# Score maxima of an attention kernel: half of a PSUM tile reduced by itself, and a few DMAs queued behind others

## The chip, the cores and the metric

The kernel runs on one core of a Trainium2 chip. The metric is the device time of one execution in microseconds (us), the lower the better. The core has TensorE (PE, with its weight loads shown as PEld), VectorE (DVE), ScalarE (ACT), GpSimd (POOL), and SyncE (SP), which here issues all the DMAs. Each engine works through its own instruction stream; semaphores order the streams against each other.

## The reference

A layer norm, grouped-query attention and a feed-forward with ternary weights, on x of 8 batches by 1024 tokens by 256 features, all in float32. There are 16 query heads and 4 key heads of 16 features each.

```python
q = rope(ln(x) @ Wq);  k = rope(ln(x) @ Wk);  v = ln(x) @ Wv
scores = einsum("bhqd,bhkd->bhqk", q, k) / sqrt(256)
p = softmax(scores)                      # over 1024 keys
x = x + ln((p @ v) @ Wo)
x = x + ln(ln(x) @ (ternary(W) * alpha).T + bias)
```

A softmax needs the largest score of each query before its exponentials can be taken safely. The kernel finds the true maxima by computing the scores twice: once to find the maxima, and once, transposed and with the maxima subtracted, for the exponentials.

## The kernel before, in words

**Blocks.** The 8192 tokens are cut into 16 units of 512 queries. A unit has 4 blocks, so there are 64 blocks, numbered `i`; a block is 512 queries of four heads (in the last unit, 128 queries of all sixteen) against all 1024 keys. `k_st` holds the stacked keys of a batch in three rotating buffers, `q_st` the stacked queries of a unit in two. Each is split in a high and a low float32r part, stacked over 64 partition rows; two heads lie in the two halves of the 128 partitions, so that a matmul over rows 0 to 63 and one over rows 64 to 127 can run side by side.

**Maxima.** `max_scores(v)` (L558) emits the maxima's matmul number `v`, of 2048. Two of them (`part` 0 and 1, each 128 queries by 512 keys) fill one PSUM tile `sm` of 128 x 2 x 512 float32, one bank for each half; the pool `ps_mx` has two such tiles. After part 1 one DVE reduction (L590) takes the maximum over both halves, 1024 values for each query, into a column of `mx`. Only block 0, whose 16 tiles hold two heads rather than two halves of one, keeps two maxima for each tile (L586, into `mx_half`), because its keys arrive in two lots; they are joined at its end (L588).

**Shift rows.** When the 16 tiles of a block are reduced, `shift_split` (L597) splits the maxima into high and low parts (two small DVE instructions, L603 and L162). Later `shift_rows` (L606) transposes them on PE (`pm`), copies them on ACT (`mh`), and two DMAs (L619) put them into rows 48 and 49 and rows 112 and 113 of the block's `q_st`. There they multiply constant rows of -1 in `k_st`, so that the second score matmul subtracts the maximum. The block's exponentials cannot begin before those rows have landed.

**Exponentials.** `exp_one(s)` (L636) emits one transposed score matmul (`se`, L628; 128 keys by 512 queries, pool `ps_e` with three tiles) and one exponential on ACT (L643). There are 32 of these in a block. `av_piece` (L655) multiplies the exponentials by `v_aug` (values and a column of ones), which makes the output and the denominators.

**The order.** PE, DVE and ACT follow the program's order as written out by hand; POOL does so during the start, and later, like SP always, follows the order that the tile framework's scheduler gives it. The program's main loop goes through `windows()` (L1010): a window has 3 exponentials, or 2 at the end of a block. `window()` (L1052) emits them in turn with as many maxima matmuls: `se`, `sm`, `se`, `sm`, `se`, `sm`; then `parts_of_step` (L1029) emits pieces of other work that a table gives to this step (projection of later units, the tail of earlier ones, shift rows), and then the `av` matmuls of two windows earlier. The maxima run ahead of the exponentials by `maxima_by` (L1006), 40 to 48 matmuls. Since a window has three maxima matmuls and a tile takes two, a window often ends with one half of a tile filled, and the next window fills the other half.

**The start.** A second table (L952 to L978) gives pieces of units 1 and 2 to steps -10 to 9. The pieces that matter here: `third("kt")` (L419) rotates and splits the keys of unit 2 on POOL, sends them to DRAM in 4 DMAs (L430) and gathers them into `k_st` in 6 (`stack_keys`, L481). `stack_queries(1)` (L537) gathers the queries of unit 1 from DRAM into `q_st` with 6 DMAs of 256 KB (L542), and fills constant rows with two more (L146).

Of the kernel before, what the change touches and what calls it, by code (L numbers as in the profile page):

```python
# [8 lines left out]
F32 = mybir.dt.float32  # L9
F32R = mybir.dt.float32r  # L10
AF = mybir.ActivationFunctionType
ALU = mybir.AluOpType
AX = mybir.AxisListType
# [3 lines left out]
P = 128  # L17
# [4 lines left out]
UT = 4  # L22
# [6 lines left out]
def kernel(  # L29
# [29 lines left out]
    nc = tc.nc  # L59
# [5 lines left out]
    NK = S // P  # L65
# [9 lines left out]
    small = ctx.enter_context(tc.tile_pool(name="small", bufs=4))  # L75
# [31 lines left out]
    for src, lo, n in ((w_q, 0, D), (w_k, D, DK), (w_v, ROT, DK)):  # L107
        nc.sync.dma_start(
            out=wqkv[:, :, lo : lo + n], in_=src.rearrange("(c p) n -> p c n", p=P)
# [51 lines left out]
    def split_lo(eng, lo, src, hi):  # L161
        eng.tensor_tensor(lo, src, hi.bitcast(F32), ALU.subtract)  # L162
# [20 lines left out]
    def psum(shape, name, dtype=F32):  # L183
        if spare[0]:
            spare[0] += 1
            if spare[0] % 5 < 2:
                return ps_mx.tile(shape, dtype, tag="sm", name=name)
        return ps_e.tile(shape, dtype, tag="se", name=name)
# [360 lines left out]
    mx = {}  # L549

    def block_queries(i, r2=slice(None)):

        u, j = divmod(i, G)
        if u < NU - 1:
            return q_st[u % 2][:, j, r2, :]
        return q_st[u % 2][:, :, r2, j * P : (j + 1) * P]

    def max_scores(v):  # L558


        i, k = divmod(v // 2, 2 * NK)
        u, part = i // G, v % 2
        if i == 0:
            a, ch, t, r2 = 1 - part, k // NK, k // 2 % UT, k % 2
        else:
            a, ch, t, r2 = 1 - k % 2, part, k // 4, k // 2 % 2
        queries = block_queries(i, r2)
        queries = queries[:, t * P : (t + 1) * P] if u < NU - 1 else queries[:, t]
        if part == 0:
            sm[0] = ps_mx.tile([P, 2, 512], F32, tag="sm", name=f"sm_{i}_{k}")  # L570
            if k == 0:
                mx[i] = small.tile([P, 2, UT, 2], F32, tag="mx", name=f"mx_{i}")
            if k == 0 and i == 0:
                mx["half"] = small.tile([P, 2, 2, UT, 2], F32, tag="mx0", name="mx_half", bufs=1)
        rows = slice(64 * a, 64 * a + 64)
        nc.tensor.matmul(  # L576
            sm[0][:, part, :],
            queries[rows],
            k_st[(u // UPB) % 3][rows, r2, ch * 512 : (ch + 1) * 512],
            start=True,  # L580
            stop=True,
        )
        if part == 0:
            return
        if i == 0:
            nc.vector.tensor_reduce(mx["half"][:, ch, ::-1, t, r2], sm[0], AX.X, ALU.max)  # L586
            if k == 2 * NK - 1:
                nc.vector.tensor_tensor(mx[0], mx["half"][:, 0], mx["half"][:, 1], ALU.max)  # L588
        else:
            nc.vector.tensor_reduce(mx[i][:, a, t, r2 : r2 + 1], sm[0], AX.XY, ALU.max)  # L590
        if k == 2 * NK - 1:
            shift_split(i)
            due.append((v // 4 + (1 if i < 2 else 2), i))

    sm, mhl = {}, {}

    def shift_split(i):  # L597

        m = mx.pop(i)
        hl = mhl[i] = small.tile([P, 2, 2, 2 * UT], F32R, tag="mhl", name=f"mhl_{i}")  # L600
        order = "(r t)" if i // G < NU - 1 else "(t r)"
        hi, lo = (hl[:, :, l].rearrange(f"p a {order} -> p a t r", r=2) for l in range(2))
        nc.vector.tensor_copy(hi, m)  # L603
        split_lo(nc.vector, lo, m, hi)

    def shift_rows(i):  # L606

        hl = mhl.pop(i)
        pm = psum([8 * UT, P], f"pm_{i}", F32R)
        nc.tensor.transpose(pm, hl.rearrange("p a l x -> p (a l x)"), ident_r)  # L610
        mh = work.tile([8 * UT, P], F32, tag="mh", name=f"mh_{i}")
        nc.scalar.copy(mh, pm.bitcast(F32))
        n = 4 * UT
        for a in range(2):
            row = 64 * a + NROW
            dst = block_queries(i)[row : row + 2].bitcast(F32)
            if len(dst.shape) == 4:
                dst = dst.rearrange("l j c t -> l (j c) t")
            nc.sync.dma_start(out=dst, in_=mh[n * a : n * a + n, :])  # L619


    es, av_ps, av_sb, d_av = {}, {}, {}, {}
# [13 lines left out]
    def exp_one(s):  # L636

        n, (a, r2) = s // 4, divmod(s % 4, 2)
        i, kt = divmod(n, NK)
        e = es[n, r2, a] = ep.tile([P, UQ], F32, tag="e", name=f"e_{i}_{kt}_{r2}_{a}")  # L640
        sc = ps_e.tile([P, 512], F32, tag="se", name=f"se_{i}_{kt}_{r2}_{a}")
        exp_scores(n, r2, a, sc)
        nc.scalar.activation(e, sc, AF.Exp, scale=1.0 / D**0.5)  # L643

    def exp_two(n, r2):

        i, kt = divmod(n, NK)
        sc = ps_mx.tile([P, 2, 512], F32, tag="sm", name=f"se_{i}_{kt}_{r2}")
        for a in range(2):
            exp_scores(n, r2, a, sc[:, a, :])  # L650
        for a in range(2):
            e = es[n, r2, a] = ep.tile([P, UQ], F32, tag="e", name=f"e_{i}_{kt}_{r2}_{a}")
            nc.scalar.activation(e, sc[:, a, :], AF.Exp, scale=1.0 / D**0.5)
# [17 lines left out]
    def av_out(i):  # L671

        u, j = divmod(i, G)
        a = av_sb[u, j] = avp.tile([P, UQ], F32, tag="avsb", name=f"avsb_{i}")
        if i < NU * G - 1:
            nc.scalar.copy(a, av_ps[0])
        else:
            half = UQ // 2
            nc.scalar.copy(a[:, :half], av_ps[0][:, :half])
            nc.vector.tensor_copy(a[:, half:], av_ps[0][:, half:])  # L680
        if u < NU - 1:
            if j == 0:
                d_av[u] = dram.tile([H, 32, UQ], F32, tag="d_av", name=f"d_av_{u}")
            nc.sync.dma_start(out=d_av[u][HKV * j : HKV * (j + 1)], in_=a)
# [199 lines left out]
    def at(step, f, *args):  # L884
        assert step >= -START
        todo.setdefault(step, []).append((f, args))
# [59 lines left out]
    def second(name, *args):  # L946
        return lambda: getattr(projects[1], name)(*args)

    def third(name, *args):
        return lambda: getattr(projects[2], name)(*args)  # L950

    for k, fs in enumerate((  # L952
        [second("x", 1, 0), second("x", 1, 1), second("kv", 0)],
        [second("kv", 1), (pick, "q", 0, 0, 1), (pick, "q", 0, 1, 1), second("v"),
         second("rotate_k"), second("split_k")],
        [(pick, "q", 1, 0), (keep_warm, 1)],
        [(keep_warm, 3), second("k"), (keep_warm, 4), (pick, "k", 1, 0), (pick, "k", 1, 1),
         (keep_warm, 2)],
        [(pick, "q", 1, 1), second("q_product", 0), third("stats", 0),
         third("norm", 0, nc.scalar)],  # L960
        [second("q_product", 1), third("stats", 1), third("hi", 0, nc.scalar), third("lo", 0),
         (pick, "q", 2, 0)],
        [(pick, "q", 2, 1), third("norm", 1, nc.scalar), third("hi", 1, nc.scalar),
         third("lo", 1), (keep_warm, 3), (fill_constant_parts, 1)],
        [third("x", 0, 0), (pick, "q", 3, 0), (keep_warm, 3)],
        [third("x", 0, 1), (pick, "q", 3, 1), second("rotate_q", 0), (keep_warm, 2)],
        [third("x", 1, 0), third("x", 1, 1), second("split_q", 0)],
        [third("kv_and_dram"), second("rotate_q", 1)],
        [third("v"), second("split_q", 1), second("q_to_dram")],
        [third("kt")],  # L970
        [],
        [(fill_constant_parts, 2)],
        [],
        [third("q", 0)],
        [],
        [third("q", 1), (stack_queries, 1)],
        [third("q_to_dram")],
    )):  # L978
        for f in fs:
            at(k - START, *(f if isinstance(f, tuple) else (f,)))  # L980
# [25 lines left out]
    def maxima_by(s):  # L1006

        return s + 4 * START + 2 * sum(s >= k for k in (28, 36, 52, 68))
# [18 lines left out]
    maxima = [0]  # L1027
# [24 lines left out]
    def window(i, s, size, late):  # L1052
        if done:
            av_out(done.pop())
        if late:
            for r2 in range(2):
                exp_two(s // 4, r2)
        else:
            end = min(maxima_by(s + size), 4 * NSTEP)
            for q in range(max(size, end - maxima[0])):  # L1060
                if q < size:
                    exp_one(s + q)
                if maxima[0] < end:
                    max_scores(maxima[0])
                    maxima[0] += 1
        behind.append((i, s, size))
        for n in range(s // 4, (s + size) // 4):
            parts_of_step(n)
        av_windows(1 if late else 2)
# [135 lines left out]
```

## Time and profile before

| | |
|---|---|
| median of three runs | 1734.97 us (1734.68 to 1735.65) |
| the profiled execution's own time | 1735.28 us |
| its span, first to last instruction | 1733.1 us |
| mean granted TensorE clock | 0.983 |
| PE busy / DVE busy / ACT busy / POOL busy | 1602.1 / 1398.1 / 1271.0 / 836.0 us |
| maxima reductions on DVE (L590) | 1008, 1190.5 us busy, 1218 ns each |
| maxima matmuls (L576) / exponentials' score matmuls (L628) | 2048 / 2048 |
| exponentials on ACT (L643) | 2000, 1055.9 us busy, 602 ns each |

"Busy" is the time in which at least one instruction of the engine was under way. Two matmuls over different halves of the rows can be under way at once, so a PE that looks busy can still be held up: a stalled matmul over one half of the rows is hidden by another that is running over the other half. Idle time is therefore only a part of what PE loses. A waiting line such as "A <- B" gives the time in which A's engine had nothing under way until B released it; PEld lines are of the weight load that stands ahead of a matmul.

### The profile page before, as it was taken

To read this page: it belongs to the slowest core of one execution; us is meant where nothing else is said; L and a number is where in the kernel's file an instruction comes from. 1 tells how busy PE (TensorE), PEld (TensorE's weight loads), DVE (VectorE), ACT (ScalarE), POOL (GpSimd) and SP (SyncE) were. 2 spreads that over 40 slices of the span, in tenths; PEclk is the share of its full clock that TensorE was granted. 3 is DMA by queue.
4 is the path that set the end of the run, shared out by engine and by line. 5 is a ranking of instruction groups with operands and counts; after the bars stand their busy time and mean duration, and the time that the engine had idled before them with its cause. 6 is when DMAs were issued, how large, how long until landed. Compare 5 with 4: busy or idle time off the path is not lost.

```text
span 1733.1 us, 35758 instructions
## 1 busy us (share of the span) xinstructions
PE 1602.1 (92%) x14200; PEld 834.1 (48%) x14200; DVE 1398.1 (81%) x1752; ACT 1271.0 (73%) x2479; POOL 836.0 (48%) x1239
## 2 busy tenths in 40 slices
PE   7969999999999999999999999999999999999997
PEld 5534454444544445454454544545454544444444
DVE  6848778888788888878888788888978887888874
ACT  4637777777687777868777777877777786877775
POOL 5522447274453637346374644737455362333354
PEclk8879999999999999999999999999999999999999
DMA  4330424225151332515124151412414141140100
GB/s 131 66 78 32 83 73 87 63 76 97 41 101 43 82 82 61 104 39 98 51 74 96 54 102 46 90 58 78 84 48 95 45 87 51 33 82 32 40 14 25
DMA packets 86071, 117.88 MB, mean 68 GB/s; under 512 B 12089, under 2 KB 50809, under 8 KB 85753
## 3 DMA queue, kind: packets, MB, share of 16 engines
q1 hardware_dynamic: 85904, 115.60, 28.9%
q8 instruction: 112, 1.84, 0.5%
q14 instruction: 55, 0.44, 0.1%
HBM read 68.65 MB, written 45.88 MB: 66 GB/s over the span
## 4 chain that ended last, share of the span: by engine, by line
PE 34%; DVE 13%; POOL 4%; ACT 4%; issue 1%; DMA 1%; SPq 0%; POOLq 0%; ACTq 0%; DVEq 0%
PE av L663 13%; DVE mx L590 10%; PE se L628 10%; PE sm L576 4%; ACT e L643 3%; PE pa L283 2%; PE pf L283 1%; PE pq L283 1%; PE pt_ot L267 1%; DMA dq<-hlq 1%; DVE bnst L237 1%; PE pkv L283 1%; PE pt_xt L267 1%; POOL hlq L162 1%; DVE mhl L603 0%
## 5 line engine op out<-in xcount | busy, mean ns | idle before, releaser
L590 DVE TENSOR_REDUCE mx<-sm 128x1 f32<-128x1024 f32 x1008 | 1190.5, 1218 | 285.5 <-PE sm L576 242.2
L643 ACT ACTIVATE e<-se 128x512 f32<-128x512 f32 x2000 | 1055.9, 602 | 301.3 <-PE sm L576 238.5
L576 PE MATMUL sm<-k_st,q_st 64*128 64x512 f32 x2048 | 736.2, 449 | 45.7 <-DVE mx L590 41.8
L628 PE MATMUL se<-q_st,k_st 64*128 64x512 f32 x2048 | 685.8, 434 | 19.3 <-DMA q_st<-mh 18.3
L663 PE MATMUL av<-e,v_aug 128*32 128x256 f32 (+3 forms) x8096 | 591.7, 392 | 0.0
L628 PEld LDWEIGHTS se<-q_st,k_st 64*128 64x128 f32 x2048 | 330.8, 186 | 368.3 <-ACT e L643 217.3
L576 PEld LDWEIGHTS sm<-k_st,q_st 64*128 64x128 f32 x2048 | 324.5, 186 | 156.7 <-DVE mx L590 125.0
L663 PEld LDWEIGHTS av<-e,v_aug 128*32 128x32 f32 x8096 | 184.3, 109 | 192.6 <-issue 145.7
L241 POOL TENSOR_SCALAR lnsc<-mv 128x2 f32<-128x2 f32 (+1 forms) x134 | 25.8, 193 | 453.6 <-DVE mv L239 448.7
L737 POOL TENSOR_TENSOR xn<-xn,a 128x512 f32<-128x512 f32 x30 | 38.4, 1280 | 129.0 <-DMA a<-d_rec 115.1
L798 POOL TENSOR_TENSOR a<-a,bias_bc 128x512 f32<-128x512 f32 x30 | 39.0, 1300 | 117.2 <-ACT a L797 117.2
L242 POOL TENSOR_TENSOR lnsc<-lnsc,mhalf 128x2 f32<-128x2 f32 (+1 forms) x134 | 92.9, 694 | 0.9
L162 POOL TENSOR_TENSOR hl<-xn,hl 128x512 fp32r<-128x512 f32 x60 | 76.4, 1285 | 0.5
L253 POOL TENSOR_SCALAR xn<-x,lnsc 128x256 f32<-128x256 f32 x116 | 64.9, 568 | 3.4
L297 POOL TENSOR_TENSOR t<-q_rot,sin_q_sb 128x512 f32<-128x512 f32 x31 | 39.7, 1282 | 32.1 <-ACT q_rot L439 32.1
L764 ACT COPY a<-pa 128x512 f32<-128x512 f32 x30 | 17.6, 586 | 45.6 <-issue 45.6
L283 PE MATMUL pq<-xt,wqkvh 128*128 128x256 f32 x256 | 46.1, 304 | 2.8 <-ACT e L643 2.8
L237 DVE BATCH_NORM_STATS2 bnst<-a 128x6 f32<-128x256 f32 x120 | 44.6, 413 | 4.7 <-POOL a L798 4.7
L283 PE MATMUL pa<-woh,hl 128*128 128x256 f32 x240 | 47.0, 298 | 0.2 <-ACT e L643 0.2
L237 DVE BATCH_NORM_STATS2 bnst<-x 128x6 f32<-128x256 f32 x124 | 45.9, 412 | 1.1 <-DMA x<-in_L_attn_x 1.1
L267 PE MATMUL pt_xt<-ident_r,xs 128*128 128x128 f32 x256 | 33.4, 260 | 12.7 <-ACT e L643 11.1
L283 PEld LDWEIGHTS pq<-xt,wqkvh 128*128 128x128 f32 x256 | 36.3, 197 | 14.6 <-ACT e L643 13.2
(156 smaller groups left out, 1320.0 us busy)
## 6 DMA issues: line engine op xcount, KB each, us to landing
q_st<-dq SPq DMA_DIRECT2D x90, 256.0 KB
dq<-hlq SPq DMA_DIRECT2D x60, 256.0 KB
d_av<-avsb SPq DMA_DIRECT2D x60, 256.0 KB
x<-in_L_attn_x SPq DMA_DIRECT2D x15, 512.0 KB
xn<-d_av SPq DMA_DIRECT2D x30, 256.0 KB
a<-d_rec SPq DMA_DIRECT2D x30, 256.0 KB
xr<-in_L_attn_x SPq DMA_DIRECT2D x15, 512.0 KB
out_x<-a SPq DMA_DIRECT2D x30, 256.0 KB
```

The lines of the kernel that those rows point to most:

```text
L162: eng.tensor_tensor(lo, src, hi.bitcast(F32), ALU.subtract)
L237: nc.vector.bn_stats(st[:, t, :], src[:, t, :])
L242: nc.gpsimd.tensor_tensor(sc[:, 1, :], sc[:, 1, :], mhalf[:, :n], ALU.pow)
L253: eng.tensor_scalar(dst[:, t, :], src[:, t, :], sc[:, 0, t : t + 1] if eng is nc.gpsimd else mv[:, t, 0:1], sc[:, 1, t : t + 1], ALU.add i ...
L267: nc.tensor.transpose(pt[:, c, t * P : (t + 1) * P], src[:, t, c * P : (c + 1) * P], ident_r)
L283: nc.tensor.matmul(out, chunk(left[i], c), chunk(right[j], c), start=(k == 0), stop=(k == len(steps) - 1),)
L297: eng.tensor_tensor(dst, x, table.unsqueeze(1).to_broadcast(list(x.shape)), ALU.mult)
L576: nc.tensor.matmul(sm[0][:, part, :], queries[rows], k_st[(u // UPB) % 3][rows, r2, ch * 512 : (ch + 1) * 512], start=True, stop=True,)
L590: nc.vector.tensor_reduce(mx[i][:, a, t, r2 : r2 + 1], sm[0], AX.XY, ALU.max)
L628: nc.tensor.matmul(sc if len(queries.shape) == 2 else sc.rearrange("p (j t) -> p j t", j=G), k_st[(i // G // UPB) % 3][rows, r2, kt * P : ...
L643: nc.scalar.activation(e, sc, AF.Exp, scale=1.0 / D**0.5)
L663: nc.tensor.matmul(av_ps[0][32 * r : 32 * r + 32, lo:hi], va[:, kt, r, :], es[i * NK + kt, r // 2, r % 2][:, lo:hi], start=(kt == 0 and lo ...
```

## The change

It has two edits.

**A half tile by itself.** At the end of a window, when the newest `sm` tile has only its first half filled, DVE reduces this half at once (`reduce_early`, which calls `reduce_halves` up to half 1). After the second half is filled, only that one is reduced. Tiles that are filled within one window are still reduced by one instruction over 1024 values, but now along one axis, to two maxima. So `mx` of every block keeps two maxima, as block 0's did before, and `shift_split` joins them in one more DVE instruction (`mc`). Block 0's own tiles are never split.

**DMAs queued.** `third("kt")` moves from step 2 to step 7 of the starting table, and `kt` and `stack_queries(1)` are traced inside `tc.issue_after(shifts[1])`, where `shifts[1]` is the second of the DMAs that write the shift rows of block 1. It orders the DMAs inside it behind that one in SP's queue, without waiting for it to land.

```diff
@@ max_scores
             if k == 0:
-                mx[i] = small.tile([P, 2, UT, 2], F32, tag="mx", name=f"mx_{i}")
-            if k == 0 and i == 0:
-                mx["half"] = small.tile([P, 2, 2, UT, 2], F32, tag="mx0", name="mx_half", bufs=1)
+                mx[i] = small.tile([P, 2, 2, UT, 2], F32, tag="mx", name=f"mx_{i}")
+            reduced.clear()
...
         if i == 0:
-            nc.vector.tensor_reduce(mx["half"][:, ch, ::-1, t, r2], sm[0], AX.X, ALU.max)
-            if k == 2 * NK - 1:
-                nc.vector.tensor_tensor(mx[0], mx["half"][:, 0], mx["half"][:, 1], ALU.max)
+            nc.vector.tensor_reduce(mx[i][:, ch, ::-1, t, r2], sm[0], AX.X, ALU.max)
         else:
-            nc.vector.tensor_reduce(mx[i][:, a, t, r2 : r2 + 1], sm[0], AX.XY, ALU.max)
+            reduce_halves(i, k, 2)
...
+    def reduce_halves(i, k, n):
+        lo = len(reduced)
+        a, t, r2 = 1 - k % 2, k // 4, k // 2 % 2
+        nc.vector.tensor_reduce(mx[i][:, lo:n, a, t, r2], sm[0][:, lo:n, :], AX.X, ALU.max)
+        reduced.extend(range(lo, n))
+
+    def reduce_early(v):
+        i, k = divmod(v // 2, 2 * NK)
+        if i > 0 and v % 2:
+            reduce_halves(i, k, 1)
...
     def shift_split(i):
-        m = mx.pop(i)
+        halves = mx.pop(i)
+        m = small.tile([P, 2, UT, 2], F32, tag="mc", name=f"mc_{i}")
+        nc.vector.tensor_tensor(m, halves[:, 0], halves[:, 1], ALU.max)
...
-            nc.sync.dma_start(out=dst, in_=mh[n * a : n * a + n, :])
+            shifts[i] = nc.sync.dma_start(out=dst, in_=mh[n * a : n * a + n, :]).ins
...
+    def behind_shift(i, f, *args):
+        with tc.issue_after(shifts[i]):
+            f(*args)
...
-        [third("kt")],
+        [],
         [],
         [(fill_constant_parts, 2)],
         [],
         [third("q", 0)],
-        [],
-        [third("q", 1), (stack_queries, 1)],
+        [(behind_shift, 1, third("kt"))],
+        [third("q", 1), (behind_shift, 1, stack_queries, 1)],
@@ window, after the se and sm matmuls
                     maxima[0] += 1
+            reduce_early(maxima[0])
         behind.append((i, s, size))
```

More of the change, by code (lines that the diff above doesn't have):

```diff
@@ L593, in max_scores @@
             due.append((v // 4 + (1 if i < 2 else 2), i))
-    sm, mhl = {}, {}
+    def reduce_halves(i, k, n):
[7 more added lines that the diff above has]
+            reduce_halves(i, k, 1)
+    sm, mhl, shifts, reduced = {}, {}, {}, []
     def shift_split(i):
-        m = mx.pop(i)
+        halves = mx.pop(i)
+        m = small.tile([P, 2, UT, 2], F32, tag="mc", name=f"mc_{i}")
+        nc.vector.tensor_tensor(m, halves[:, 0], halves[:, 1], ALU.max)
         hl = mhl[i] = small.tile([P, 2, 2, 2 * UT], F32R, tag="mhl", name=f"mhl_{i}")
```

## Prediction

> **What bounds the kernel now.** I read the page first, then the list of waits, then the timeline of plain windows. Engines, costliest groups:
>
> ```profile
> PE 1602.1 (92%) x14200; PEld 834.1 (48%) x14200; DVE 1398.1 (81%) x1752; ACT 1271.0 (73%) x2479; POOL 836.0 (48%) x1239
> ...
> L590 DVE TENSOR_REDUCE mx<-sm 128x1 f32<-128x1024 f32 x1008 | 1190.5, 1218 | 285.5 <-PE sm L576 242.2
> ```
>
> PE is the busiest, but DVE's idle time (285.5 us) is mostly waiting for a maxima matmul. Waits, in total, times, longest:
>
> ```profile
> PEld sm L576 <- DVE mx L590: 125.0, 204, 2.3
> ...
> PE sm L576 <- DVE mx L590: 41.8, 119, 1.8
> ...
> PE se L628 <- DMA q_st<-mh: 18.3, 8, 13.0
> ```
>
> So PE and DVE wait for each other: a loop. Timeline of two plain windows (start, us, engine, line, [idle before]); A fills tile 0 and half of tile 1, B the rest of tile 1 and tile 2:
>
> ```profile
> 804.85 0.49 PE L576 MATMUL sm<-k_st,q_st 64*128 64x512 f32 x1
> ...
> 805.64 1.23 DVE L590 TENSOR_REDUCE mx<-sm 128x1 f32<-128x1024 f32 x1 [0.86 <-PE sm L576]
> 805.73 0.86 PE L663 MATMUL av<-e,v_aug 128*32 128x256 f32 x16
> ...
> 806.52 0.50 PE L576 MATMUL sm<-k_st,q_st 64*128 64x512 f32 x1
> ...
> 806.92 0.50 PE L576 MATMUL sm<-k_st,q_st 64*128 64x512 f32 x1
> ...
> 807.09 3.49 DVE L590 TENSOR_REDUCE mx<-sm 128x1 f32<-128x1024 f32 x3 [0.23 <-PE sm L576]
> ```
>
> A starts at 804.84, B at 806.52 (A takes 1.68), the next at 808.36 (B takes 1.84). DVE begins tile 0 0.80 after A's start, ends at 806.87, and idles 0.23 for the second half of tile 1. PE goes on 0.04 after DVE frees a tile (806.87 to 806.92).
>
> From the trace's PE instructions I cut all windows and timed each window in which a split tile begins (A) and the one after it (B). "Unstalled" takes off what the stretch of score matmuls has over its undisturbed 0.89:
>
> - 253 pairs with a plain A: A 2.04 (1.68 unstalled), B 2.12 (1.89 unstalled); 102 of these pairs run at full speed, under 3.6 together.
> - 29 with a transpose in A: A 2.85 (2.13), B 2.98 (2.65).
> - 30 with long work in A: A 4.72 (3.55).
>
> The start has one large stall besides (timelines of SP's queue and of PE):
>
> ```profile
> 84.44 3.07 SPq L430 DMA_DIRECT2D dk<-ks  x4
> ...
> 93.42 2.30 SPq L542 DMA_DIRECT2D q_st<-dq  x5
> 96.23 1.41 SPq L619 DMA_DIRECT2D q_st<-mh  x2
> ```
>
> ```profile
> 105.85 0.94 PE L628 MATMUL se<-q_st,k_st 64*128 64x512 f32 x2 [13.01 <-DMA q_st<-mh]
> ```
>
> The shift rows of block 1 are ready on ACT at 87.45 (copy at 87.19 for 0.26), but stand behind 15 DMAs of keys and queries.
>
> [...] here the granted clock is 0.5 from 97.8 to 118.3.
>
> **The change, part by part.**
>
> *1. A new wait.* The instruction order of the changed kernel (PE's own order of work is unchanged) shows 313 tiles split, 695 not, and what each matmul waits for. In before, a tile's second matmul never waits for DVE: only its first does, for the tile to be free. In the changed one all 313 second matmuls of split tiles wait for DVE, and the count they wait for is that of **the early reduction of the same tile's first half**. The framework orders by tile, not by bank. Behind that matmul stand, in PE's order, the rest of B's scores and its `av`; behind those, ACT.
>
> When is it met? With A starting at 0: DVE begins tile 0 at 0.80; its next reduction follows 1.17 later (three in 3.49); the half takes 0.68. Nearest row, a reduction of 512 from SBUF:
>
> ```profile
> L203 DVE TENSOR_REDUCE part<-fw x1: 676/676/676, 126.4 to 126.4; 128x1 f32<-128x512 f32 x1
> ```
>
> With 0.04 to pass it on: 0.80 + 1.17 + 0.68 + 0.04 = 2.69. Bounds on the half: 0.61 (half of 1.218) and 0.70, so 2.62 to 2.71. A plain A is over at 1.68. So PE stands for 1.0 us where it ran undisturbed, and A effectively becomes 2.69. In return the older stalls go: once the half is done, tile 0 is free, and B runs at its unstalled length. Plain pairs: 253 x (2.69 + 1.89 - 2.04 - 2.12) = +106 us. Transpose pairs: 29 x (2.69 + 2.65 - 2.85 - 2.98) = -14. Long A: the wait is hidden (3.55 > 2.69), and their stall comes from other DVE work, which stays: 0, at best 30 x (3.55 - 4.72) = -35. Together **+92**.
>
> *2. DVE's extra work.* 313 more reductions at 2 x 0.68 - 1.22 = 0.14 give 44 us, already inside the 2.69 and hidden after it: DVE stands 0.55 while the released matmul runs. 63 more joins `mc` at 0.33 (the mean of the splits L603 and L162, with operands of the same size) are 21 us; half of them follow a reduction that PE waits for: +10, bounds 0 and 21. What is late next: 122 groups of layer norm statistics (two of 0.41, two of 0.17, some 1.1) that now fall between the early half and the next full tile. After B's matmul DVE needs 0.55 + 0.68 + 1.17 = 2.40, and the next window wants it at 0.80 + 0.79 + 0.80 = 2.39: no slack but the window's other work. I take +0.2 of each, +24, bounds 0 and 0.5 each.
>
> PE's waits for itself on 311 first matmuls look back six matmuls or more: 0, covered by those matmuls[...].
>
> *3. The DMAs.* On SP's queue, the shift rows of block 1 (2 DMAs) move ahead of `dk` (4), `k_st` (6), `q_st<-dq` (6) and the fill of `q_st` (2). Before them are then only the four `dq<-hlq`, issued from 78.17 to 82.95. The rows are issued at about 87.5 to 88.9; `d_k`, issued at 70.70, let its reader be issued at 73.06, 2.4 later, so they land near 91.3, before PE asks at 92.84. The 13.0 go, and some of the half-clock work after it (12.2 us from 105.8 to 118.0): -16, bounds -13 and -19. POOL: `kt` keeps its place ahead of unit 2's query rotation; only two of its multiplications pass behind a split of queries (L157, L162): 0. The moved DMAs end some 6 us later; their queries are first read by block 4's maxima, at 151.6 in before. Even 30 us would be covered; without that cover, PE would wait for them directly.
>
> Sum against the profiled execution: 1735.3 + 92 + 10 + 24 - 16 = **1845**. The runs' median is 0.3 lower, which changes nothing here. A measurement can tell about 0.2% from no change.
>
> **The rivals.**
>
> *R1, the gap is filled and the wait is met (faster).* DVE's idle 0.23 to 0.70 in each pair goes, as the diff's words suggest. It decides where the half is done by 2.5 after A's start: at 2.5, plain pairs cost 253 x 0.23 = 58, less 14, less the 35 of long A, less 16: about 0. For it: 167 us of PE and PEld waiting on DVE, and B's stalls. Against it: 2.62 even with the cheapest half, before the joins. If the wait cost nothing, a gain of 0.33 in 253 pairs, and 16: 1735 - 83 - 16 = 1636. Chance 0.05.
>
> *R2, the wait hides, but DVE is the bound.* Its added 44 + 21 us lie on the path: 1735 + 65 - 16 = 1784. For it: DVE runs three reductions back to back in plain windows. Against it: the new wait makes DVE idle 0.55 in each pair. Chance 0.12.
>
> *R3, both cancel.* Long A lose all their stall, the half takes 0.61, joins and statistics cost nothing: 1845 - 35 - 20 - 34 = 1756; no change needs yet another 21. Chance 0.02.
>
> *R4, the old stalls stay beside the new one.* B keeps 253 x 0.23 + 29 x 0.33 = 67, statistics cost 0.5 each (+37): 1949. Chance 0.11.
>
> Main case (1845): 0.70.
>
> **How the numbers follow.** Slower is the main case, R2 and R4: 0.93; same 0.02; faster 0.05. R3 with the cheap ends of the main case reaches 1756, R4 1949; leaving out the outer tenths of the chance gives 1770 to 1925.
>
> **What would show it.** Right: second halves of `sm` head PE's waits on DVE, some 280 of about 0.5 to 1.0 us in place of 125.0; half reductions of 0.66 to 0.70; A and B together some 4.6 in plain pairs; DVE idle 0.5 before the second half; no 13 us wait near 93. PE's idle time rises by over 100 us, DVE's busy time to about 1463. Wrong: if second halves start within 1.7 of a plain A's start, the new wait is no wait, and the sum falls to R1; if DVE runs without gaps through plain windows, it is R2; if a long wait for `q_st` appears before block 4, part 3 fails.

## The result, and the profile after

The changed kernel takes 1825.25 us (median of 4 runs, 1823.64 to 1826.31) against 1734.83 for the kernel before (4 runs, 1727.35 to 1735.65). The ratio is 1.053, 95% interval 1.050 to 1.056: 90 us slower. The profiled execution took 1823.64, its span is 1821.9; the span before was 1733.1, so the two traces have 88.8 us to explain.

The page, engines and costliest groups (busy, mean ns of one | idle before, releaser):

```profile
PE 1647.0 (90%) x14200; PEld 840.6 (46%) x14200; DVE 1430.6 (79%) x2128; ACT 1297.8 (71%) x2479; POOL 834.5 (46%) x1239
...
L596 DVE TENSOR_REDUCE mx<-sm 128x1 f32<-128x512 f32 (+1 forms) x1321 | 1220.5, 966 | 339.1 <-PE sm L575 307.2
```

The groups of DVE with their shapes kept apart show the two kinds of reduction:

```profile
L596 DVE TENSOR_REDUCE mx<-sm 128x2 f32<-128x1024 f32 x695 | 838.8, 1218 | 139.2 <-PE sm L575 109.9 <-PE se L640 19.0
L596 DVE TENSOR_REDUCE mx<-sm 128x1 f32<-128x512 f32 x626 | 428.9, 685 | 199.9 <-PE sm L575 197.3 <-PE se L640 2.6
```

695 tiles are whole, 313 are split. DVE does only 32 us more work, yet it waits 307 us for maxima matmuls where it waited 242. The list of waits (total, times, longest) says whom PE waits for:

```profile
PEld sm L575 <- DVE mx L596: 241.8, 384, 2.3
...
PE sm L575 <- DVE mx L596: 113.5, 232, 1.9
```

The first line has nearly doubled and the second nearly tripled (125.0 and 41.8 before). Both engines wait more, for each other, which points to an order and not to added work; the experiments test that. Here is the same tile as in the two windows that the prediction showed, in the changed kernel (timeline: start, us, engine, line, [idle before]):

```profile
830.87 0.49 PE L575 MATMUL sm<-k_st,q_st 64*128 64x512 f32 x1
...
831.67 1.82 DVE L596 TENSOR_REDUCE mx<-sm 128x2 f32<-128x1024 f32 x2 [1.18 <-PE se L640]
...
832.55 0.50 PE L640 MATMUL se<-q_st,k_st 64*128 64x512 f32 x1
833.55 0.19 PEld L575 LDWEIGHTS sm<-k_st,q_st 64*128 64x128 f32 x2 [0.82 <-DVE mx L596]
833.55 0.50 PE L575 MATMUL sm<-k_st,q_st 64*128 64x512 f32 x2 [0.50 <-DVE mx L596]
...
834.08 1.82 DVE L596 TENSOR_REDUCE mx<-sm 128x1 f32<-128x512 f32 x2 [0.59 <-PE sm L575]
```

A starts at 830.87. DVE takes the full tile and then the half, ending at 833.49; only then, at 833.55, does PE fill the other half, 2.68 after A's start. Before, it did so at 1.68. Then DVE has nothing to do for 0.59. The next window starts at 835.22: the pair takes 4.35 us, where it took 3.52.

Measured in this way on all pairs of windows (sums over the same 312 pairs in both traces):

| | before | after | change |
|---|---|---|---|
| 253 pairs with a plain A | 1053.5 | 1180.8 | +127.3 |
| 29 with a transpose in A | 168.8 | 163.9 | -4.9 |
| 30 with long work in A | 226.5 | 197.6 | -28.9 |
| all other windows, start and end | 284.3 | 279.5 | -4.8 |
| span | 1733.1 | 1821.9 | +88.8 |

The start, on SP's queue and on PE (timelines of the changed kernel):

```profile
88.78 1.41 SPq L631 DMA_DIRECT2D q_st<-mh  x2
90.29 2.35 SPq L430 DMA_DIRECT2D dk<-ks  x4
```

```profile
92.58 0.75 PE L640 MATMUL se<-q_st,k_st 64*128 64x512 f32 x2
```

The shift rows of block 1 go out ahead of the key and query DMAs, at 88.78 in place of 96.23, and block 1's first score matmul runs at 92.58 in place of 105.85, without a wait.

### The profile page after: what moved, and what is told of

It reads as the page before. It is cut to its first block, busy times and chain, and to the rows that moved or that the text cites. A ratio compares the mean times of both kernels' runs of the same rounds, so it can differ in the third digit from the quotient of the medians.

```text
span 1821.9 us, 36123 instructions
## 1 busy us (share of the span) xinstructions
PE 1647.0 (90%) x14200; PEld 840.6 (46%) x14200; DVE 1430.6 (79%) x2128; ACT 1297.8 (71%) x2479; POOL 834.5 (46%) x1239
## 4 chain that ended last, share of the span: by engine, by line
PE 52%; DVE 34%; ACT 5%; issue 3%; DMA 2%; POOL 2%; SPq 1%; POOLq 0%; ACTq 0%; DVEq 0%
DVE mx L596 29%; PE se L640 16%; PE av L675 15%; PE sm L575 10%; ACT e L655 4%; PE pa L283 3%; PE pq L283 2%; PE pf L283 2%; PE pkv L283 1%; PE pt_xt L267 1%; DVE bnst L237 1%; PE pt_ot L267 1%; DVE mc L611 1%; DVE mhl L615 1%; DVE mhl L162 1%
## 5 line engine op out<-in xcount | busy, mean ns | idle before, releaser
L596 DVE TENSOR_REDUCE mx<-sm 128x1 f32<-128x512 f32 (+1 forms) x1321 | 1220.5, 966 | 339.1 <-PE sm L575 307.2
L655 ACT ACTIVATE e<-se 128x512 f32<-128x512 f32 x2000 | 1082.6, 601 | 379.5 <-PE sm L575 255.5
L575 PE MATMUL sm<-k_st,q_st 64*128 64x512 f32 x2048 | 646.9, 452 | 118.0 <-DVE mx L596 113.5
L640 PE MATMUL se<-q_st,k_st 64*128 64x512 f32 x2048 | 702.0, 430 | 3.5 <-DMA q_st<-mh 2.1
L640 PEld LDWEIGHTS se<-q_st,k_st 64*128 64x128 f32 x2048 | 341.9, 185 | 364.7 <-ACT e L655 244.2
L575 PEld LDWEIGHTS sm<-k_st,q_st 64*128 64x128 f32 x2048 | 279.9, 185 | 257.7 <-DVE mx L596 241.8
L810 POOL TENSOR_TENSOR a<-a,bias_bc 128x512 f32<-128x512 f32 x30 | 38.6, 1288 | 166.9 <-ACT a L809 166.7
L162 POOL TENSOR_TENSOR hl<-xn,hl 128x512 fp32r<-128x512 f32 x60 | 76.5, 1288 | 0.5
L776 ACT COPY a<-pa 128x512 f32<-128x512 f32 x30 | 17.6, 586 | 36.5 <-issue 35.7
L267 PE MATMUL pt_ot<-ident_r,hl 128*128 128x128 f32 x240 | 31.1, 253 | 13.1 <-ACT e L655 13.1
```

What stands on the lines that cost most here:

```text
L267: nc.tensor.transpose(pt[:, c, t * P : (t + 1) * P], src[:, t, c * P : (c + 1) * P], ident_r)
L575: nc.tensor.matmul(sm[0][:, part, :], queries[rows], k_st[(u // UPB) % 3][rows, r2, ch * 512 : (ch + 1) * 512], start=True, stop=True,)
L596: nc.vector.tensor_reduce(mx[i][:, lo:n, a, t, r2], sm[0][:, lo:n, :], AX.X, ALU.max)
L640: nc.tensor.matmul(sc if len(queries.shape) == 2 else sc.rearrange("p (j t) -> p j t", j=G), k_st[(i // G // UPB) % 3][rows, r2, kt * P : ...
```

## The experiments

**Theory:** the second half of a split tile stands for DVE's reduction of the first half, though the halves share no element of the tile; this order alone makes the kernel slow. **Rivals:** DVE's added work is on the path (R2); the half reductions gain nothing even when they are free; the DMA edit does harm.

The edits are shown shortened. The kernel before was run beside each set: 1733.48 (e1 to e4), 1734.95 (e5 to e8), 1737.04 (e9) and 1731.21 (e10 and e11). A difference between runs of different sets is therefore good to some 5 us.

### e1: the second half freed

The changed kernel, where the framework is told that the two instructions don't depend on each other.

```diff
+            early = nc.vector.tensor_reduce(...)          # half 1 of a split tile
...
+        mm = nc.tensor.matmul(sm[0][:, part, :], ...)
+            tc.declare_no_dep(mm.ins, reduced_early[0].ins, reason="the halves lie in two banks")
```

> The changed kernel, with the wait of each split tile's second matmul on the early reduction of its first half taken out; the two lie in different PSUM banks. All else stays: half reductions, joins, DMA order. Theory (the wait costs the time): DVE's gaps are filled and PE runs on, 1640 to 1740 us, likeliest 1690, faster than before; second halves start 1.7 us after a plain A's start, not 2.7. Rival R2 (DVE's extra work is the bound): 1784 or more. If the wait is not the cause at all: 1825.

Measured: **1707.98 us** (1695.66 to 1709.54), ratio 0.984 (0.980 to 0.988). That is 117 us under the changed kernel and 25 under the one before (1733.48 in these runs). The second half of plain pairs starts 1.70 after A's start (median); their sum falls from 1180.8 to 1026.0. The same tile in this kernel's timeline:

```profile
785.50 0.50 PE L575 MATMUL sm<-k_st,q_st 64*128 64x512 f32 x1
...
786.30 3.55 DVE L599 TENSOR_REDUCE mx<-sm 128x2 f32<-128x1024 f32 x4 [1.40 <-PE sm L575]
...
787.18 0.49 PE L575 MATMUL sm<-k_st,q_st 64*128 64x512 f32 x1
```

The second half starts at 787.18, 1.68 after A, while DVE is still busy with the full tile, and DVE runs four reductions without a gap. The next window starts at 789.02: 3.52 us for the pair, as before. So the wait is the cause: with it gone, and all else as in the changed kernel, the loss is gone too. The gain that R1 hoped for exists, but only without this order.

The order belongs to the framework's tracking of tiles. Here 234 of the 313 second halves overlap DVE's reading of the first half by 0.2 us or more. These reductions take 0.68 us in the median, as where nothing overlaps; the matmuls take 0.50 in both cases, though the profile models the ends of matmuls. In the freed kernel, for example, the first of the two matmuls of this PE line fills a second half from 505.15 to 505.65, while the second of the four reductions of the DVE line reads the first half from 505.34 to 506.02:

```profile
505.15 0.82 PE L575 MATMUL sm<-k_st,q_st 64*128 64x512 f32 x2
```

```profile
504.26 3.48 DVE L599 TENSOR_REDUCE mx<-sm 128x2 f32<-128x1024 f32 x4
```

### e2 and e3: each edit alone

e2 is the kernel before with `behind_shift` and the moved `kt` only. e3 is the changed kernel with these taken back:

```diff
-        [],
+        [third("kt")],
...
-        [(behind_shift, 1, third("kt"))],
-        [third("q", 1), (behind_shift, 1, stack_queries, 1)],
+        [],
+        [third("q", 1), (stack_queries, 1)],
```

> Before, with the DMA edit alone. Theory: the 13.0 us wait of block 1's first score matmul goes, and with it part of the half-clock stretch: 13 to 19 us under before, about 1719. Rival (the transfer is hidden elsewhere, or the moved DMAs are missed later): within 3 us of before, with a new wait on q_st or k_st between 90 and 200 us.

> Before, with the half-tile edit alone. Theory: the wait does the same harm without the DMA edit, and the 13 us stall is back: 1838 to 1844. Rival (the two edits interact, and the reordering of DMAs is what slowed the rest): clearly under 1825.

Measured: e2 **1721.72** (ratio 0.993, 0.991 to 0.995), e3 **1836.30** (1.060, 1.057 to 1.062). The DMA edit is worth 12 us alone and 11 with the halves; the halves cost 103. Both runs lie 1 to 2 us outside what was expected of them, e2 with a little less gain and e3 with a little less loss; neither reaches the rival's figure.

### e4 and e5: DVE's extra work without the early start

e4 reduces the 313 tiles in two halves as well, but both after the tile is full, so there is no new wait. e5 only keeps two maxima for each tile and joins them. No DMA is moved in either.

```diff
 e4, against e3, in max_scores, after part 1 (apart[0]: a window ended with this tile half filled;
 reduce_early only sets it)
+            if apart[0]:
+                reduce_halves(i, k, 1)
             reduce_halves(i, k, 2)
 e5, against e3
-            reduce_early(maxima[0])
```

> Before, with the same 313 tiles reduced in two halves and the joins, but both halves after the tile is full: DVE has all the extra instructions, and no matmul waits for a half. Theory: most of the extra 0.14 us for each split tile and the joins show, since DVE is in PE's loop: 1755 to 1790, likeliest 1775. Rival R2 (the extra DVE work alone explains the slowdown): about 1840, as slow as the half-tile edit alone. If the extra work is hidden: 1735.

> The kernel before, with every block's maxima kept as two (one for each half of the keys) and joined by one more DVE instruction, 63 more; no tile is split and no DMA moves. It divides the 37 us that the late halves cost without any wait. If the joins are the dear part[...]: 1755 to 1765. If they cost what the prediction put down, 63 x 0.33 us with half of it on the path: 1735 + 10 = 1745, at most 1756. Then the other 27 us are of the 313 added reductions. If they are hidden: 1735.

Measured: e4 **1770.75** (ratio 1.020, 1.018 to 1.023), e5 **1752.85** (1.009, 1.006 to 1.012). Without the wait DVE's extra work costs 37 us, so it can't alone explain the 103 of e3 (R2 asked for about 1840): some 18 for 63 joins (0.28 each) and the rest for 313 added reductions. So e1's 25 is a balance: 12 from the DMAs, 37 lost to DVE's work, and by difference some 50 won by starting the first halves early. No single run shows these 50.

### e6 and e7: the wait made shorter, and moved onto other work

If the wait sets the time, then the time must follow the moment of release. e6 lets the early reduction take 256 of the 512 columns, and the second one the other 768. e7 is the kernel before, nothing split, in which the second matmul of those 313 tiles waits for the reduction of the *previous* tile.

```diff
 e6, in reduce_halves
+        if n - lo == 1:
+            part = (slice(0, 256), slice(256, 1024))[lo]
+            flat = sm[0].rearrange("p c t -> p (c t)")[:, part]
+            nc.vector.tensor_reduce(mx[i][:, lo, a, t, r2 : r2 + 1], flat, AX.X, ALU.max)
 e7, in max_scores
+        if held[0]:
+            tc.add_manual_dep(mm.ins, last[0].ins.name, ...)    # last: the reduction before
```

> As the halves alone (no DMA moved), but the early reduction takes 256 of the first half's 512 columns and the second takes the other 768: as many DVE instructions as before, a shorter wait. Theory (the second half of the tile stands for the early reduction): [...]about 0.42 us in place of 0.685, so second halves start 0.80 + 1.17 + 0.42 + 0.04 = 2.43 us after a plain A's start, not 2.68, and A + B lose up to 0.26 in 253 + 29 pairs, up to 73 us against the halves alone (1836): 1765. The longer second reduction leaves DVE only 0.02 us of slack in a pair, so some comes back: 1765 to 1810, likeliest 1785. Rival (what costs is the number of DVE's instructions or their work, not the wait for the early one): as the halves alone, 1830 to 1840.

> The kernel before, with nothing split and no DVE work added; only the second matmul of each of the 313 tiles waits for DVE's reduction of the tile before. A wait in the same place that is met 0.6 us earlier. Theory (a wait costs what it holds PE beyond a plain A's 1.68, and in return removes later stalls): released at 0.80 + 1.22 + 0.04 = 2.06 after A's start; the sum of A and B goes from 4.17 to at most 2.06 + 1.89 + 0.23 = 4.18 where pairs were stalled already, and up by 0.4 to 0.5 in the 102 pairs that ran at full speed: 1735 + 20 to 45, 1755 to 1780, likeliest 1765. Rival (a wait at this place costs about 1 us wherever it is released, since it breaks PE's row of matmuls): 1735 + over 80 = 1815 or more.

Measured: e6 **1810.51** (1.044, 1.041 to 1.046), e7 **1777.96** (1.025, 1.023 to 1.027). The groups of e6 with shapes apart:

```profile
L599 DVE TENSOR_REDUCE mx<-sm 128x1 f32<-128x768 f32 x313 | 299.5, 957 | 215.2 <-PE sm L575 213.7 <-PE se L645 1.5
L599 DVE TENSOR_REDUCE mx<-sm 128x1 f32<-128x256 f32 x313 | 129.3, 413 | 0.0
```

As many instructions as in e3, and 0.27 off the early one (0.413 us, where a straight line through the 0.685 of 512 columns and the 1.218 of 1024 gives 0.42). e6 gains 26 us over e3, half of the likeliest 51 and at the dear end of its range. e7 does no added DVE work and still loses 43 us, as expected. The same tile in e7's timeline, released 2.08 after A's start at 814.84:

```profile
815.64 1.22 DVE L597 TENSOR_REDUCE mx<-sm 128x1 f32<-128x1024 f32 x1 [0.86 <-PE sm L576]
...
816.92 0.50 PE L576 MATMUL sm<-k_st,q_st 64*128 64x512 f32 x2
```

Over all plain pairs the order is strict:

| | second half starts after A's start, median | sum of 253 plain pairs | run |
|---|---|---|---|
| e8, freed | 1.70 | 1021.3 | 1717.68 |
| before | 1.86 | 1053.5 | 1734.83 |
| e7 | 2.24 | 1096.8 | 1777.96 |
| e6 | 2.42 | 1138.0 | 1810.51 |
| e3 | 2.68 | 1180.8 | 1836.30 |

From e6 to e3 the release moves by 0.26 us and the pairs by 0.17 each; the rest is covered. Both rivals fall: at the same number of DVE instructions the time differs, and a wait at this place doesn't cost a fixed sum.

### e8: the freed halves without the DMA edit

The edit of e1 upon e3.

> The halves alone (no DMA moved), with the second matmul of a split tile freed from the wait for the early reduction of the first half, which lies in another bank. If the wait and the DMAs add up without touching each other: 1836 - 117 = 1719, that is the freed kernel's 1708 and the 12 us of the DMAs, 1712 to 1726. If the DMAs' gain hung on the halves: within 1700 to 1710 or over 1730.

Measured: **1717.68** (0.990, 0.988 to 0.991), 119 below e3 and 10 above e1. Wait and DMAs add up.

### e9, e10, e11: less small work on DVE

e9 is e1 with the join written straight into the high part of the shift rows, the low part left at zero. e10 does the same in the changed kernel, with its wait; e11 in the kernel before, where it saves one instruction of a block, not two.

```diff
+        nc.vector.memset(hl[:, :, 1].bitcast(F32), 0.0)      # once, for each of three buffers
...
-        m = small.tile([P, 2, UT, 2], F32, tag="mc", name=f"mc_{i}")
-        nc.vector.tensor_tensor(m, halves[:, 0], halves[:, 1], ALU.max)
-        nc.vector.tensor_copy(hi, m)
-        split_lo(nc.vector, lo, m, hi)
+        nc.vector.tensor_tensor(hi, halves[:, 0], halves[:, 1], ALU.max)
```

> The changed kernel with the freed second half (1708 us), and the join writes the rounded maxima straight into the high part of the shift rows; the low part is set to zero once. So the copy into the high part and the subtraction for the low part are left out, two small DVE instructions of each block, 128 of them, 47 us busy in the freed kernel. A softmax may subtract any number near the maximum, since numerator and denominator hold the same factor. Theory (the small DVE instructions at a block's end lie mostly on the path, as 63 added joins cost 18 us for 26 us busy): 0.7 x 47 = 33 us less, 1675, between 1665 and 1690. Rival ([...]little goes): 1695 to 1708.

> The changed kernel as it is, its second halves waiting, with the zero low part: two small DVE instructions of each block left out, 128 in all, 28 us busy in the changed kernel. It asks how much of DVE's small work lies on the path while PE waits for the halves, a term the prediction set at one half. If one half: 14 us less, 1811. If the wait covers them (DVE stands idle in each pair anyhow): 1820 to 1828. If they cost as much as without the wait, where leaving them out gave 60: 1765.

> The kernel before with the zero low part: nothing split, no DMA moved, no join; one small DVE instruction of each block is left out (the subtraction, 64, 21.5 us busy before). If each small instruction lies on the path with somewhat more than its busy time, as in the freed kernel (60 us for 128, 0.47 each): 30 less, 1705. If it is only 0.28 each, as the added joins were: 18 less, 1717. If the gain in the freed kernel needed the halves: 1735. It also tells what the halves are worth without small instructions: 1648 against this one.

Measured: e9 **1648.09** (0.950, 0.947 to 0.952), e10 **1805.02** (1.041, 1.039 to 1.043), e11 **1712.21** (0.990, 0.986 to 0.993). e9 is the best version of all, 89 us under the kernel before (1737.04 in these runs), and it missed its expectation: 60 us came from 128 instructions (0.47 each), where 33 were expected. e10 gained 20 from as many (0.16 each; the one half of their busy time that was assumed is 14), e11 some 19 from 64 (0.30 each). So where PE stands for the halves, two thirds of what this work costs without the wait is covered. The waits of e9:

```profile
PEld sm L575 <- DVE mx L599: 48.4, 112, 1.5
```

In e1 that was 87.8; the wait of PE itself for `mx`, 38.0 in e1, is 4.4. Some 6 of e9's 60 us are gained by the 20th window. In e1, PE there waits 2.0 for the small split and then runs at half the granted clock from 60 to 70 us (0.51); in e9 that wait isn't there, and the clock in these 10 us is 1.00.

How can 128 instructions that were busy for 47 us be worth 60? By pairs of windows, 35 of the 61 us between the two traces lie in the 30 pairs with long work in A, and 18 in the 253 plain ones. This is one of the long windows in e1:

```profile
205.93 2.52 POOL L162 TENSOR_TENSOR hl<-xn,hl 128x512 fp32r<-128x512 f32 x2
206.05 1.20 DVE L620 CAST mhl<-mc 128x16 fp32r<-128x16 f32 x1
...
207.28 1.22 DVE L162 TENSOR_TENSOR mhl<-mc,mhl 128x16 fp32r<-128x16 f32 x1
...
209.67 0.79 PE L575 MATMUL sm<-k_st,q_st 64*128 64x512 f32 x1 [1.66 <-DVE mx L599]
```

Two small instructions beside POOL's large ones hold DVE for 2.4 us, PE is idle for 1.66, and from 209.7 on the granted clock is 0.5 for 3.4 us. The twelve `pa` matmuls that follow take 2.9 us; in e9 the same twelve, at the full clock, take 1.7. After the first 200 us, e1's trace has 13 such half-clock stretches, 51 us together, 8 of them in long windows. The trace of e9 has two (7 us), that of the kernel before two (7 us), of e4 nine (41 us), of the changed kernel none. So in this window more was lost than the two instructions' own time: the twelve matmuls after them took 1.2 us longer, at the lower clock. How the 60 us divide between the two was not measured by a run of its own.

## Why the prediction was right

The forecast was slower, 1845; measured 1825, inside 1770 to 1925. Its main case is what happened. Its sum over the kernel before was +110; the spans show +88.8.

| step | predicted | measured |
|---|---|---|
| half reduction | 0.68 (0.61 to 0.70) | 0.685 |
| release after A's start | 2.69 | 2.68 (median) |
| plain pairs, wait | +106 | +127 together |
| joins and statistics | +10 and +24 | in the line above |
| transpose pairs | -14 | -5 |
| long A | 0 (at best -35) | -29, of which 14 is the start's stall (e2) |
| DMAs | -16 (-13 to -19) | -10 to -12 in the medians (e2, e3, e8), -17.6 in e2's trace |

**The new wait.** Right in its kind, place and time: e1 shows that it is worth 117 us. Both lengths in the sum held. In the mean of the 253 plain pairs the second half starts 2.76 after A's start (2.69 predicted), and from there to the end of B it takes 1.90 (1.89 predicted). With the joins and the statistics the forecast put these pairs at +140, and they came to +127. The 13 us lie in the terms of DVE's other work: the later release and the longer B leave some 22 us for joins, statistics and all else, where 34 were set down. How these 22 divide was not measured.

B's 1.90 is a mean of two kinds: 1.61 in the 153 pairs whose B holds no other PE work, 2.35 in the 100 where it does (transposes, products). In both, B's first exponential score (832.55 in the timeline) does not wait and runs during the stall. So PE does not stand for the whole wait, which the forecast's "PE stands for 1.0 us" overlooks.

The medians of pairs with no statistics and no small split in them, 3.53 before and 4.36 after, say what was given back. At this difference 253 pairs would lose 210 us. They lost 127, so 83 came back, as the forecast's "In return the older stalls go" has it.

**Joins.** e10's 0.16 for a small instruction gives an estimate of 10 us for 63 joins in the changed kernel, the prediction's value. Without the wait they cost 18 (e5), near the upper bound of 21.

**The DMAs.** The rows landed in time, as said, and no long wait for `q_st` came later: block 4's first maxima matmul ran at 140.2, before at 151.6. From 85 to 135 us the granted clock is one half for 27.3 us before and for 10.2 in the changed kernel. In the medians the gain is 10 to 12 us, just below the lower bound. In the two traces it is 17 by the time that the kernel before is at 201.3 (e2 is there at 184.5), and still 17.6 at the end (1733.1 to 1715.5): e2's profiled execution was the fastest of its four, 1717.46 us where the slowest took 1725.19. Whether 16 was too much can't be told within this spread.

**The signs that the prediction named.** Half reductions, DVE's idle of 0.5 (0.59), A and B of 4.6 (4.67 in the mean) and the vanished 13 us wait came true. So did the waits of second halves: 256 of them wait for DVE in the weight load, 0.81 us in the median, and none did before. Two signs did not. PE's idle time was to rise by over 100 us; it rose from 131.0 to 174.9. The rest of the loss lies in PE's busy time, 45 us more for the same 14200 matmuls. Before, `se` and `sm` ran side by side over the two halves of the rows, in one stretch of busy time. Now B's first `se` runs alone (832.55), for the same 0.50, and two `sm` run together after the wait (833.55). Over the whole trace, `se` and `sm` are under way at the same time for 609 us before and for 482 after. The groups agree: `sm` is 646.9 us busy where it was 736.2, as `sm` now overlaps `sm`, and `se` 702.0 where it was 685.8. DVE's busy time was to be 1463 and is 1430.6. Reductions that follow each other overlap at their ends in the records (1008 of 1218 ns make 1190.5 us), so the added ones brought 30, not 44; and the small splits, 42.5 us before, shrank to 27.8.

**The rivals.** R2 (DVE is the bound) would have needed the wait to hide; without it, DVE's 65 us of work cost 37 (e4). R1 (the wait is met) put a free half at 83 us of gain. Where it is free, in e8, it gains 17, after the 37 that DVE's work takes back; and in the changed kernel it isn't met. R4's old stalls did not stay: after the release B takes 1.90, its unstalled length, and not the 2.12 that it took before.

## What to carry to other kernels

Before splitting a buffer's reader to start it earlier, look at what the *next writer* of that buffer waits for: where the framework tracks the whole tile, an early read of one half makes the writer of the other half stand for it (here 256 of them, 0.81 us in the median), and two engines that overlapped now take turns. Price it as release time less the time at which the writer could have run, in a plain window, and then see which later stalls it returns. If the parts really are independent, say so to the framework (separate tiles would be another way, not tried here); here that turned 5% slower into 1.6% faster, and three small instructions made one, in the same loop, gave another 3.4%.

## What the runs showed of the hardware

A small DVE instruction had no fixed price here. The join and the splits, over 16 elements, in the changed kernel (one tile's instructions: duration ns, min/median/max):

```profile
L611 DVE TENSOR_TENSOR mc<-mx x64: 174/176/1102, 54.6 to 1766.2; 128x16 f32<-128x16 f32 x64
L615 DVE CAST mhl<-mc x64: 174/182/1208, 55.8 to 1766.4; 128x16 fp32r<-128x16 f32 x64
```

The median is 0.18 us and the longest 1.2, about the time of one large POOL instruction (1288 ns for `hl` in the changed kernel). The traces tie the two together. In the changed kernel 20 of the 192 joins and splits take over 0.3 us, and each of these ends 30 to 45 ns after a POOL instruction that it overlapped. Of the 172 shorter ones, three overlap any POOL instruction. In e1 it is 42 of 192, each ending 21 to 52 ns after a POOL instruction. No run here took POOL's work away, so what makes the two end together is not shown. Overlap alone isn't enough: in e1, 33 of the 150 shorter ones overlap a POOL instruction too, mostly a small one. The same cast has a mean of 224 ns in the changed kernel and 410 in e1, with as many POOL instructions in both (1239). So their number does not set it; that the timing of the work around it does is a reading that no run tested.

Some short pauses of PE were followed by a lower clock. From 200 to 1640 us, PE in e1 is idle for 90 us in all and 17 times for 1.4 us or more (at most 2.5); 11 of these 17 pauses are followed by 3.4 or 6.8 us at a granted clock of one half. In the changed kernel PE is idle for more, 127 us in all, but only once for over 1.4 us, and the clock stays whole. In the kernel before, with 86 us of idle time, one of three such pauses (1.54, at 1456.3) is followed by 3.4 us at one half, and the only other half-clock stretch there, at 746.3, comes after a pause of 1.19. So between these kernels the lost clock doesn't go with the sum of the idle time; it goes with the long pauses, though not with every one. What sets it was not shown.
